# A four-layer image network on one core: layer 3's last sum one pair later, search's sum over its own row of norms, and the freed room as load buffers

## The chip, the cores and the metric

The kernel runs on one core of one Trainium2 chip. The metric is device time in microseconds (us), from the first to the last instruction with what lies around them; less is better. The core has five engines with an instruction stream each, executed in order: TensorE (PE, matmul; PEld is its weight load), VectorE (DVE), ScalarE (ACT), GpSimd (POOL) and SyncE (SP, which here only issues transfers). They meet through semaphores. Matmuls write to PSUM, a small memory of eight banks of 512 float32 per partition; everything else lives in SBUF, and large arrays in HBM.

## What is computed

Sixteen images of 64 x 64 tokens with 256 channels, in float32, go through four layers. Each normalises its input over 32 groups of channels (`_gn`), computes something and adds it to the input.

```python
# layer 0: nearest of 1024 codes
dis = sum(xf*xf) + sum(e*e) - 2*xf@e;  x = x + e.T[argmin(dis)]
# layer 1: attention within each row of 64 tokens, sigmoid instead of softmax
attn = sigmoid(einsum('bhik,bhjk->bhij', x@Wf+bf, x@Wg+bg));  x = x + attn @ (x@Wh+bh)
# layer 2: a gate per token from a softmax over 4096 tokens of a rank-one product
sim = x0[:, :, None]*x1[:, None, :];  feats = einsum('bn,bnm->bm', x2, softmax(sim, axis=1))
x = x + sigmoid(feats) * x
# layer 3: linear attention with 4 heads of 32, a projection, a layer norm over channels
q = softmax(q over d)*32**-0.5;  k = softmax(k over n)
out = (context(k, v) applied to q) @ w_out + b_out
x = x + layernorm(out)*gamma + beta
```

## The kernel before

Every image passes through stages, written as Python generators that yield after a piece of work: `stats0` (group statistics of the input), `stage1` (the search of layer 0), `layer1`, `rows2` and `stage2` (layer 2: its three rows, then the exponentials), `gate2` (the gate) and `stage3` (layer 3). A list of tasks with start times and lengths merges the generators of several images, so that the search of one image, layer 1 of another, the exponentials of a third, and gate and layer 3 of older ones run beside each other. That merged order only sets priorities: a tile library then schedules the instructions engine by engine by its own estimate of when each is ready, hands out the buffers of its pools, and puts in all semaphores. So the number of buffers under a tag sets not only what may be in flight but also the final order on each engine. Between stages the activations go through HBM, in chunks of 512 tokens (512 KB each; eight chunks per image).

What the change touches, with the line numbers of the profile:

- **The shared load buffers `xb`** (L57), three of them. Four stages load chunks into them on SP's queue: the statistics (xs, L293), the rows of layer 2 (xr, L562), the keys and values of layer 3 (xk, L732) and its output pass (xo, L846). `rows2` takes eight chunks in two halves of four; each chunk is read by two matmuls (L565); after a half, ACT copies the rows (L569), TensorE transposes them (L574) and DVE stores the two columns (L575) that `stage2` needs to begin.
- **The tag `t4`** in the pool `s1p`, five buffers of 4 KB per partition: the negated norms nn (L372), the sums nd (L384), the squares sq of the search's normalisation (L325), the projections fg of layer 1 (L464), the rows of layer 2 (L569), and a constant at the start.
- **The search** per token tile of 128: ACT forms nn = minus the norms (L372); TensorE makes the products with the 1024 codes in a two-bank PSUM tile pd (L377, four matmuls); DVE adds both into nd and takes the maximum (L384), then finds its place (L389, FIND_INDEX8); POOL gathers the code and adds it to the tokens (L390).
- **The gate** (`gate2`), per chunk: SP loads the chunk xg (L665) and a row gb of gates, the same for all partitions (L667, one buffer); ACT makes the factors u (L674), DVE multiplies (L675); SP stores (L681). The gates reach HBM by a transfer on ACT's queue (L641).
- **Layer 3's output pass**, per chunk of four tiles, two pairs each. `form` loads the queries qo (L824, tag `qo`, two buffers) and makes a product (L826, L828); `variance` reduces it to the layer norm's scale (L834, L836, L837). For each pair TensorE makes po (L854); ACT scales it into y (L857); TensorE transposes the input into the PSUM bank px and adds a row (L859, L863); DVE adds px and y (L865). When a chunk's second pair is done, the first pair of the next chunk stores it (L867; the last chunk at L872). The y tiles have two buffers.
- **PSUM**: the pool `ps_m` has four banks, taken in turn by nearly all small products of all stages (po, px, pz, pvr, pr, pt, pk, pqv, pfg, psc and more); `ps_w` has two double banks for pd, ph and po of layer 1.

Of the kernel before, what the change touches and what calls it, by code (L numbers as in the profile page):

```python
# [9 lines left out]
F32 = mybir.dt.float32  # L10
# [3 lines left out]
ALU = mybir.AluOpType  # L14
AX = mybir.AxisListType

P = 128
C = 256
NK = C // P
# [4 lines left out]
CW = CH * P  # L24
# [3 lines left out]
CODES = 1024  # L28
CK = 32
# [12 lines left out]
def kernel(  # L42
# [7 lines left out]
    nc = tc.nc  # L50
# [3 lines left out]
    const = ctx.enter_context(tc.tile_pool(name="const", bufs=1))  # L54
    xa = ctx.enter_context(tc.tile_pool(name="xa", bufs=3))
    xm = ctx.enter_context(tc.tile_pool(name="xm", bufs=3))
    xb = ctx.enter_context(tc.tile_pool(name="xb", bufs=3))  # L57
    xg = ctx.enter_context(tc.tile_pool(name="xg", bufs=2))
    s1p = ctx.enter_context(tc.tile_pool(name="s1p", bufs=2))
    s2p = ctx.enter_context(tc.tile_pool(name="s2p", bufs=1))  # L60
    s3p = ctx.enter_context(tc.tile_pool(name="s3p", bufs=2))
# [33 lines left out]
    dmat = const.tile([P, P], F32, name="dmat")  # L95
    nc.vector.tensor_tensor(dmat, ident, gmat, ALU.subtract)
    hmask = blocks("hmask", DH, 1.0)
    neg_mat = s1p.tile([P, P], F32, tag="t4", name="neg_mat", bufs=5)
    nc.vector.memset(neg_mat, -1.0)
    neg32 = const.tile([P, 32], F32, name="neg32")  # L100
    nc.vector.memset(neg32, -1.0)
# [201 lines left out]
    def stage1(b):  # L303
        tag = f"s1_{b}"
        scale, _, nbias = norm0.pop(b)
        src = xT[b].rearrange("(k p) n -> p k n", p=P)
        tok = x[b].rearrange("(t p) c -> p t c", p=P)
        xt, xc, xn, nx2, pxt = {}, {}, {}, {}, {}

        def load(ch):  # L310
            xt[ch] = xa.tile([P, NK, CW], F32, tag="xa", name=f"xt_{tag}_{ch}")
            nc.sync.dma_start(out=xt[ch], in_=src[:, :, ch * CW : (ch + 1) * CW])

        def tokens(ch):
            xc[ch] = s1p.tile([P, CH, C], F32, tag="xc", name=f"xc_{tag}_{ch}")
            nc.sync.dma_start(out=xc[ch], in_=tok[:, ch * CH : (ch + 1) * CH, :])

        def norm(ch):
            xn[ch] = s1p.tile([P, NK, CW], F32, tag="xn", name=f"xn_{tag}_{ch}")
            sq = s1p.tile([P, NK, CW], F32, tag="t4", name=f"sq_{tag}_{ch}", bufs=5)  # L320
            for k in range(NK):
                nc.scalar.activation(
                    xn[ch][:, k, :], xt[ch][:, k, :], AF.Identity, bias=nbias[:, k : k + 1], scale=scale[:, k : k + 1]
                )
                nc.scalar.activation(  # L325
                    sq[:, k, :], xt[ch][:, k, :], AF.Square, bias=nbias[:, k : k + 1], scale=scale[:, k : k + 1]
                )
            px = bank(f"px_{tag}_{ch}")
            for t in range(CH):
                for k in range(NK):  # L330
                    nc.tensor.matmul(
                        px[32 * t : 32 * t + 32, :P], lhsT=neg32, rhs=sq[:, k, t * P : (t + 1) * P],
                        start=(k == 0), stop=(k == NK - 1),
                    )
            xrow = small.tile([P, P], F32, tag="xrow", name=f"xrow_{tag}_{ch}", bufs=1)
            nc.scalar.copy(xrow, px[:, :P])
            pxt[ch] = bank(f"pxt_{tag}_{ch}")
            nc.tensor.transpose(pxt[ch][:, :P], xrow, ident)

        def norm_rows(ch):  # L340
            px = pxt.pop(ch)
            nx2[ch] = small.tile([P, CH], F32, tag="x2", name=f"nx2_{tag}_{ch}")
            nc.vector.tensor_copy(nx2[ch], px[:, :P].rearrange("p (t n) -> p t n", n=32)[:, :, 0])  # L343

        st1 = stats_tile(1, f"st1_{tag}")
        x1_d[b] = []

        def back(ch):
            for k in range(NK):
                pt = bank(f"pt_{tag}_{ch}_{k}")  # L350
                for t in range(CH):
                    nc.tensor.transpose(
                        pt[:, t * P : (t + 1) * P], xc[ch][:, t, k * P : (k + 1) * P], ident
                    )
                nc.scalar.copy(xt[ch][:, k, :], pt)
            chunk_stats(st1, xt[ch], ch)
            d = dram.tile([P, NK, CW], F32, tag=f"x1_{ch}", name=f"x1_{tag}_{ch}")
            nc.scalar.dma_start(out=d, in_=xt.pop(ch))
            x1_d[b].append(d)

        load(0)
        load(1)
        norm(0)
        norm_rows(0)
        tokens(0)
        yield 4
        for ch in range(NCHUNK):
            for t in range(CH):
                T = ch * CH + t

                nn = s1p.tile([P, CODES], F32, tag="t4", name=f"nn_{tag}_{T}", bufs=5)
                nc.scalar.activation(nn, ne2, AF.Identity, bias=nx2[ch][:, t : t + 1])  # L372
                pd = wide(f"pd_{tag}_{T}")
                for hf in range(2):
                    cols = slice(hf * 512, (hf + 1) * 512)
                    for k in range(NK):
                        nc.tensor.matmul(  # L377
                            pd[:, cols], lhsT=xn[ch][:, k, t * P : (t + 1) * P], rhs=e2[:, k, cols],
                            start=(k == 0), stop=(k == NK - 1),
                        )  # L380

                nd = s1p.tile([P, CODES], F32, tag="t4", name=f"nd_{tag}_{T}", bufs=5)
                m8 = m8s[T % 4]
                nc.vector.tensor_tensor_reduce(  # L384
                    out=nd, in0=pd, in1=nn, scale=1.0, scalar=-3.0e38, op0=ALU.add, op1=ALU.max,
                    accum_out=m8[:, 0:1],
                )
                i8 = small.tile([P, 8], U32, tag="i8", name=f"i8_{tag}_{T}", bufs=4)
                nc.vector.max_index(i8, m8, nd)  # L389
                nc.gpsimd.indirect_dma_start(  # L390
                    out=xc[ch][:, t, :], out_offset=None,
                    in_=emb_rows, in_offset=bass.IndirectOffsetOnAxis(ap=i8[:, 0:1], axis=0),
                    compute_op=ALU.add,
                )
# [21 lines left out]
    def layer1(b):  # L416
        tag = f"l1_{b}"
        scale, nmean, _ = norm1.pop(b)
# [32 lines left out]
        def attend(ch):  # L451
            X = xt[ch]
            pfg = bank(f"pfg_{tag}_{ch}")
            HW = CW // 2
            for k in range(NK):
                for n in range(4):
# [1 line left out]
                        pfg[n * CK : (n + 1) * CK, :HW], lhsT=wfg_n[:, k, (n // 2) * CK : (n // 2 + 1) * CK],  # L458
                        rhs=X[:, k, (n % 2) * HW : (n % 2 + 1) * HW], start=(k == 0), stop=(k == NK - 1),
                    )  # L460
            fg = s1p.tile([2 * CK, 2, HW], F32, tag="t4", name=f"fg_{tag}_{ch}", bufs=5)
            for n in range(2):
                part = slice(2 * n * CK, 2 * (n + 1) * CK)
                nc.scalar.activation(fg[:, n, :], pfg[part, :HW], AF.Identity, bias=bfg_n[part, :])  # L464
# [75 lines left out]
    def rows2(b):  # L540
        tag = f"r2_{b}"
        scale, nmean, _ = norm2[b]
# [15 lines left out]
        for h in range(2):  # L558
            pr = bank(f"pr_{tag}_{h}")
            for j in range(4):  # L560
# [3 lines left out]
                for k in range(NK):  # L564
                    nc.tensor.matmul(  # L565
                        pr[part, :], lhsT=wrow_n[:, k, part], rhs=xt[:, k, :], start=(k == 0), stop=(k == NK - 1)
                    )
            rows = s1p.tile([P, CW], F32, tag="t4", name=f"rows_{tag}_{h}", bufs=5)
            nc.scalar.activation(rows, pr, AF.Identity, bias=brow_n)  # L569
            for n in range(3):  # L570
                nc.scalar.dma_start(out=rd[n, h], in_=rows[n : n + 97 : 32, :])
# [81 lines left out]
    def gate2(b):  # L653
        tag = f"g2_{b}"
        scale, nmean, _ = norm2.pop(b)
# [7 lines left out]
        for ch in range(NCHUNK):  # L663
            xt = xg.tile([P, NK, CW], F32, tag="xg", name=f"xg_{tag}_{ch}")
            nc.sync.dma_start(out=xt, in_=x2[ch])  # L665
            gb = s3p.tile([P, CW], F32, tag="gb", name=f"gb_{tag}_{ch}", bufs=1)
            nc.sync.dma_start(  # L667
                out=gb,
                in_=gd[ch * CH : (ch + 1) * CH, :].rearrange("t p -> (t p)").rearrange("(o n) -> o n", o=1)
# [19 lines left out]
    def stage3(b):  # L689
# [130 lines left out]
        qs, prods, rss = {}, {}, {}  # L820

        def form(ch):
            qs[ch] = s3p.tile([P, CW], F32, tag="qo", name=f"qo_{tag}_{ch}")
            nc.sync.dma_start(out=qs[ch], in_=qTs[ch])  # L824
            pz = bank(f"pz_{tag}_{ch}")
            nc.tensor.matmul(pz, lhsT=gram, rhs=qs[ch], start=True, stop=True)  # L826
            prods[ch] = s3p.tile([P, CW], F32, tag="v2", name=f"qz_{tag}_{ch}", bufs=4)
            nc.vector.tensor_tensor(prods[ch], pz, qs[ch], ALU.mult)  # L828
# [11 lines left out]
        yield 3  # L840
        variance(0)
        yield 3
        before = None
        for ch in range(NCHUNK):
            xt = xb.tile([P, NK, CW], F32, tag="xb", name=f"xo_{tag}_{ch}")
            nc.sync.dma_start(out=xt, in_=x3[ch])  # L846
# [2 lines left out]
            for pr in range(2):  # L849
# [11 lines left out]
                            is_transpose=True, start=(j == 0 and k == 0), stop=False, skip_group_check=True,  # L861
                        )
                nc.tensor.matmul(px, lhsT=ones3, rhs=twice(x_row), start=False, stop=True, skip_group_check=True)  # L863
                two = y[:, 2 * pr : 2 * pr + 2, :]
                nc.vector.tensor_tensor(two, px, two, ALU.add)  # L865
                if pr == 0 and before is not None:
                    nc.sync.dma_start(out=dst[:, (ch - 1) * CH : ch * CH, :], in_=before)  # L867
                if ch + 1 < NCHUNK:
                    (form, variance)[pr](ch + 1)
                yield 3  # L870
            before = y
        nc.sync.dma_start(out=dst[:, TOK // P - CH :, :], in_=before)  # L872


# [70 lines left out]
```

## Time and profile before

| | us |
|---|---|
| median of three runs | 5931.24 (5928.14 to 5945.72) |
| the profiled execution, in all | 5928.44 |
| its span, first to last instruction | 5926.7 |
| ACT ex_s (L617), 1024 times | 2137.8, mean 2088 ns |
| DVE ex_s (L620), 1024 times | 2350.7, mean 2302 ns |
| PE pd_s (L377), 4096 times | 2022.2, mean 623 ns |
| DVE sum of the search (L384), 512 times | 622.2, mean 1215 ns |
| DVE FIND_INDEX8 (L389), 512 times | 624.1, mean 1219 ns |
| ACT nn_s (L372), 512 times | 583.2, mean 1141 ns |
| DVE sum of layer 3 (L865), 256 times | 175.2, mean 686 ns |
| POOL gather (L390), 512 times | 1058.1, mean 2067 ns |

The profile is one execution on the chip. Its page gives the busy time of each engine, the span in 40 slices (a digit is the busy share in tenths; PEclk is the clock granted to TensorE, in tenths of full speed), the transfer queues, the chain of work that ended last, and groups of instructions: line, engine, operation, tile written <- tiles read, count, busy time, mean ns of one, and the idle time of the engine ahead of them with what ended it. A wait is written as the waiting engine, tile and line, then `<-` and what released it. SPq is SP's queue of transfers. Matmuls are pipelined, so a busy TensorE is not one at its peak. TensorE's 4096 pd_s here are float32 matmuls that each stand as two instructions.

The first 500 us fill the pipeline of stages, the last 600 empty it; between, the picture repeats every 351 us.

### The profile page before, as it was taken

Reading aid. Unit: us, or ns where it says so; the run is one execution under the profiler, and the core shown is the slowest. Engines: PE = TensorE matmul, PEld = TensorE weight load, DVE = VectorE, ACT = ScalarE, POOL = GpSimd, SP = SyncE. Lnnn points to the kernel's source line nnn. Section 1 sums busy time; section 2 is a strip of 40 time slices with the busy share of each in tenths; the row PEclk is TensorE's granted clock in tenths of the full one; section 3 lists DMA queues with packets and bytes.
Section 4 is the critical chain, followed back from the end, with each engine's and each line's share of the span. In section 5 each row is a group of like instructions: output and inputs, shape, how many; then the busy total and the mean of one; then the engine's idle time right before and its main releaser. Section 6 shows DMA issues by size and latency. Waiting matters only on the chain.

```text
span 5926.7 us, 79561 instructions
## 1 busy us (share of the span) xinstructions
PE 5337.4 (90%) x28239; PEld 3211.1 (54%) x28239; DVE 5121.1 (86%) x7282; ACT 4570.8 (77%) x6754; POOL 1939.4 (33%) x1314
## 2 busy tenths in 40 slices
PE   8968899889999999998989999898999989997777
PEld 3524465545656565564656556565555646564555
DVE  6499798989989898898989889898998989888882
ACT  4377687878778787887879788797878878787873
POOL 3122233224233332433334233342424333231331
PEclk9989999989999898999999899999999999998899
DMA  6544745555656656565665656656565664644543
GB/s 186 162 124 124 225 137 177 184 184 162 207 168 192 197 151 202 184 207 181 184 205 167 194 183 188 206 174 204 164 210 164 202 204 147 209 158 173 184 158 116
DMA packets 521380, 1059.47 MB, mean 179 GB/s; under 512 B 52504, under 2 KB 266392, under 8 KB 512792
## 3 DMA queue, kind: packets, MB, share of 16 engines
q1 hardware_dynamic: 406288, 885.11, 44.7%
q0 software_dynamic: 73728, 67.14, 7.9%
q10 hardware_dynamic: 40968, 102.13, 4.5%
q8 instruction: 224, 3.67, 0.3%
q14 instruction: 172, 1.41, 0.1%
HBM read 751.18 MB, written 303.04 MB: 178 GB/s over the span
## 4 chain that ended last, share of the span: by engine, by line
PE 48%; DVE 16%; ACT 12%; DMA 7%; issue 6%; POOL 4%; ACTq 0%; SPq 0%; POOLq 0%; DVEq 0%
PE pd_s L377 15%; DVE ex_s L620 6%; ACT ex_s L617 5%; PE ph_l L468 5%; PE pqv_s L759 3%; PE po_s L854 3%; PE pk_s L737 3%; PE po_l L506 2%; PE pr_r L565 2%; DMA xr_r<-x_l 2%; DVE i_s L389 2%; POOL qv_s L779 2%; PE pvr_s L834 1%; PE pz_s L826 1%; DMA qo_s<-qd_s 1%
## 5 line engine op out<-in xcount | busy, mean ns | idle before, releaser
L620 DVE CUSTOM_DVE_ANT_0 ex_s<-ex_s,x2b 128x2048 f32<-128x2048 f32 x1024 | 2350.7, 2302 | 46.2 <-ACT ex_s L617 44.9
L617 ACT ACTIVATE ex_s<-x0b,nmax_s,x_r 128x2048 f32<-128x2048 f32 x1024 | 2137.8, 2088 | 66.4 <-DVE num_s L620 60.3
L377 PE MATMUL pd_s<-e,xn_s 128*128 128x512 f32 x4096 | 2022.2, 623 | 43.5 <-DVE m L384 40.8
L390 POOL DMA_INDIRECT xc_s<-in_emb_rows,i_s x512 | 1058.1, 2067 | 2063.9 <-DVE i_s L389 1466.8
L377 PEld LDWEIGHTS pd_s<-e,xn_s 128*128 128x128 f32 x4096 | 754.4, 197 | 764.9 <-issue 669.1
L384 DVE CUSTOM_DVE_ANT_0 nd_s<-pd_s,nn_s 128x1024 f32<-128x1024 f32 x512 | 622.2, 1215 | 174.4 <-ACT nn_s L372 82.1
L389 DVE FIND_INDEX8 i_s<-m,nd_s 128x8 uint32<-128x1024 f32 x512 | 624.1, 1219 | 0.0
L372 ACT ACTIVATE nn_s<-ne,nx_s 128x1024 f32<-128x1024 f32 x512 | 583.2, 1141 | 21.5 <-DVE nx_s L343 15.7
L468 PE MATMUL ph_l<-wh_l,xt_l 128*128 128x256 f32 x2048 | 525.5, 393 | 28.3 <-DVE m L384 16.5
L759 PE MATMUL pqv_s<-wqv_s,xk_s 128*128 128x256 f32 x2048 | 494.6, 382 | 0.0
L759 PEld LDWEIGHTS pqv_s<-wqv_s,xk_s 128*128 128x128 f32 x2048 | 390.9, 192 | 127.5 <-issue 65.5
L468 PEld LDWEIGHTS ph_l<-wh_l,xt_l 128*128 128x128 f32 x2048 | 380.9, 193 | 143.8 <-issue 57.5
L837 POOL TENSOR_TENSOR lrs_s<-lrs_s,mhalf 128x4 f32<-128x4 f32 x128 | 183.0, 1429 | 749.3 <-ACT lrs_s L836 710.5
L857 ACT ACTIVATE y_s<-po_s,lrs_s 128x256 f32<-128x256 f32 x512 | 237.1, 469 | 214.8 <-PE po_s L854 166.2
L854 PE MATMUL po_s<-wctx_s,qo_s 128*128 128x256 f32 x1024 | 336.0, 415 | 32.3 <-ACT y_s L857 31.1
L506 PE MATMUL po_l<-at_l,h_l 64*128 64x64 f32 x4096 | 318.5, 297 | 46.2 <-DVE xt_l L511 42.7
L506 PEld LDWEIGHTS po_l<-at_l,h_l 64*128 64x128 f32 x4096 | 286.5, 206 | 108.5 <-DVE xt_l L511 48.9
L779 POOL TENSOR_TENSOR qv_s<-qv_s,qm_s 128x512 f32<-128x512 f32 x128 | 232.7, 1818 | 312.3 <-DVE qm_s L778 181.7
L728 POOL TENSOR_TENSOR qv_s<-qv_s,qd_s 128x512 f32<-128x512 f32 x128 | 199.8, 1561 | 304.6 <-DVE qd_s L727 252.9
L865 DVE TENSOR_TENSOR y_s<-pxo_s,y_s 128x512 f32<-128x512 f32 x256 | 175.2, 686 | 125.0 <-ACT y_s L857 123.2
L854 PEld LDWEIGHTS po_s<-wctx_s,qo_s 128*128 128x128 f32 x1024 | 178.2, 198 | 172.5 <-ACT y_s L857 84.7
L737 PE MATMUL pk_s<-xk_s,wk_s 128*128 128x512 f32 x512 | 269.6, 650 | 0.0
(195 smaller groups left out, 7519.8 us busy)
## 6 DMA issues: line engine op xcount, KB each, us to landing
xs_s<-in_xT SPq DMA_DIRECT2D x128, 512.0 KB
xt_s<-in_xT SPq DMA_DIRECT2D x128, 512.0 KB
xc_s<-in_x SPq DMA_DIRECT2D x128, 512.0 KB
x_s<-xt_s ACTq DMA_DIRECT2D x128, 512.0 KB
xt_l<-x_s SPq DMA_DIRECT2D x128, 512.0 KB
x_l<-xt_l SPq DMA_DIRECT2D x128, 512.0 KB
xr_r<-x_l SPq DMA_DIRECT2D x128, 512.0 KB
xg_g<-x_l SPq DMA_DIRECT2D x128, 512.0 KB
```

Of the source, the lines that this page charges most:

```text
L372: nc.scalar.activation(nn, ne2, AF.Identity, bias=nx2[ch][:, t : t + 1])
L377: nc.tensor.matmul(pd[:, cols], lhsT=xn[ch][:, k, t * P : (t + 1) * P], rhs=e2[:, k, cols], start=(k == 0), stop=(k == NK - 1),)
L384: nc.vector.tensor_tensor_reduce(out=nd, in0=pd, in1=nn, scale=1.0, scalar=-3.0e38, op0=ALU.add, op1=ALU.max, accum_out=m8[:, 0:1],)
L389: nc.vector.max_index(i8, m8, nd)
L390: nc.gpsimd.indirect_dma_start(out=xc[ch][:, t, :], out_offset=None, in_=emb_rows, in_offset=bass.IndirectOffsetOnAxis(ap=i8[:, 0:1], axis=0),
L468: nc.tensor.matmul(ph[:, t, :], lhsT=X[:, k, t * P : (t + 1) * P], rhs=wh_n[:, k, :], start=(t % 2 == 0 and k == 0), stop=False, skip_grou ...
L506: nc.tensor.matmul(po[:, r, k * CH + t, :], lhsT=h[rows, t, k * P : (k + 1) * P], rhs=at[rows, t, :], start=True, stop=True,)
L617: nc.scalar.activation(ex, x0b, AF.Exp, bias=nmax[:, T : T + 1], scale=x01[:, T, 1:2], accum_out=den[:, h, T : T + 1])
L620: nc.vector.tensor_tensor_reduce(out=ex, in0=ex, in1=x2b, scale=1.0, scalar=0.0, op0=ALU.mult, op1=ALU.add, accum_out=num[:, h, T : T + 1],)
L737: nc.tensor.matmul(pk, lhsT=wk_n[:, k, :], rhs=xt[:, k, :], start=(k == 0), stop=(k == NK - 1))
L759: nc.tensor.matmul(pqv[:, j, :], lhsT=xt[:, k, t * P : (t + 1) * P], rhs=wqv_n[:, k, :], start=(j == 0 and k == 0), stop=False, skip_group ...
L854: nc.tensor.matmul(po[:, j, :], lhsT=qT[:, t * P : (t + 1) * P], rhs=wctx[:, 1, :], start=True, stop=True)
```

## The change

Five edits, all in one function:

1. `xb` gets a fourth buffer.
2. The search's sum is written over nn, so that nd goes; the tag `t4` goes from five buffers to three. FIND_INDEX8 reads nn.
3. The gate row gb gets a second buffer.
4. The query tile qo gets a third buffer.
5. In layer 3's output pass the sum of px and y of a pair is issued after the matmuls of the next pair (`late`); the store of the previous chunk moves from the first pair to the second; the very last sum stands after the loop.

In SBUF, per partition: `t4` gives back 8 KB; xb takes 4, gb and qo 2 each.

```diff
-    xb = ctx.enter_context(tc.tile_pool(name="xb", bufs=3))
+    xb = ctx.enter_context(tc.tile_pool(name="xb", bufs=4))
...
-            sq = s1p.tile([P, NK, CW], F32, tag="t4", name=f"sq_{tag}_{ch}", bufs=5)
+            sq = s1p.tile([P, NK, CW], F32, tag="t4", name=f"sq_{tag}_{ch}", bufs=3)
...
-                nn = s1p.tile([P, CODES], F32, tag="t4", name=f"nn_{tag}_{T}", bufs=5)
+                nn = s1p.tile([P, CODES], F32, tag="t4", name=f"nn_{tag}_{T}", bufs=3)
...
-                nd = s1p.tile([P, CODES], F32, tag="t4", name=f"nd_{tag}_{T}", bufs=5)
                 m8 = m8s[T % 4]
                 nc.vector.tensor_tensor_reduce(
-                    out=nd, in0=pd, in1=nn, scale=1.0, scalar=-3.0e38, op0=ALU.add, op1=ALU.max,
+                    out=nn, in0=pd, in1=nn, scale=1.0, scalar=-3.0e38, op0=ALU.add, op1=ALU.max,
                     accum_out=m8[:, 0:1],
                 )
...
-                nc.vector.max_index(i8, m8, nd)
+                nc.vector.max_index(i8, m8, nn)
...
-            gb = s3p.tile([P, CW], F32, tag="gb", name=f"gb_{tag}_{ch}", bufs=1)
+            gb = s3p.tile([P, CW], F32, tag="gb", name=f"gb_{tag}_{ch}", bufs=2)
...
-            qs[ch] = s3p.tile([P, CW], F32, tag="qo", name=f"qo_{tag}_{ch}")
+            qs[ch] = s3p.tile([P, CW], F32, tag="qo", name=f"qo_{tag}_{ch}", bufs=3)
...
-        before = None
+        before = late = None
         for ch in range(NCHUNK):
...
                 nc.tensor.matmul(px, lhsT=ones3, rhs=twice(x_row), start=False, stop=True, skip_group_check=True)
-                two = y[:, 2 * pr : 2 * pr + 2, :]
-                nc.vector.tensor_tensor(two, px, two, ALU.add)
-                if pr == 0 and before is not None:
+                if late is not None:
+                    nc.vector.tensor_tensor(late[1], late[0], late[1], ALU.add)
+                late = px, y[:, 2 * pr : 2 * pr + 2, :]
+                if pr == 1 and before is not None:
                     nc.sync.dma_start(out=dst[:, (ch - 1) * CH : ch * CH, :], in_=before)
                 if ch + 1 < NCHUNK:
                     (form, variance)[pr](ch + 1)
                 yield 3
             before = y
+        nc.vector.tensor_tensor(late[1], late[0], late[1], ALU.add)
         nc.sync.dma_start(out=dst[:, TOK // P - CH :, :], in_=before)
```

The buffer count of `t4` changes from 5 to 3 in the same way at the constant, at fg and at the rows.

More of the change, by code (lines that the diff above doesn't have):

```diff
@@ L97 @@
     hmask = blocks("hmask", DH, 1.0)
-    neg_mat = s1p.tile([P, P], F32, tag="t4", name="neg_mat", bufs=5)
+    neg_mat = s1p.tile([P, P], F32, tag="t4", name="neg_mat", bufs=3)
     nc.vector.memset(neg_mat, -1.0)
@@ L460, in attend @@
                     )
-            fg = s1p.tile([2 * CK, 2, HW], F32, tag="t4", name=f"fg_{tag}_{ch}", bufs=5)
+            fg = s1p.tile([2 * CK, 2, HW], F32, tag="t4", name=f"fg_{tag}_{ch}", bufs=3)
             for n in range(2):
@@ L567, in rows2 @@
                     )
-            rows = s1p.tile([P, CW], F32, tag="t4", name=f"rows_{tag}_{h}", bufs=5)
+            rows = s1p.tile([P, CW], F32, tag="t4", name=f"rows_{tag}_{h}", bufs=3)
             nc.scalar.activation(rows, pr, AF.Identity, bias=brow_n)
```

## The prediction

> **What bounds the kernel now.** I read the page first, then the span cut into stretches, then the waits of TensorE in the steady part, then the waits of SP's own queue, then the chain of waits around one change of image and at the end. Parts 1 and 2 of the page:
>
> ```profile
> PE 5337.4 (90%) x28239; PEld 3211.1 (54%) x28239; DVE 5121.1 (86%) x7282; ACT 4570.8 (77%) x6754; POOL 1939.4 (33%) x1314
> PE   8968899889999999998989999898999989997777
> ...
> PEclk9989999989999898999999899999999999998899
> ```
>
> No engine is idle for long. The steady part repeats every 351 us (one image leaves, one enters). Two of its stretches, with a column each for PE, PEld, DVE, ACT and POOL busy, the granted clock, the DMA share and GB/s:
>
> ```profile
> 2400.00:2750.00 350.00, 325.32 (x1781) 197.76 (x1780) 320.96 (x458) 288.88 (x426) 125.15 (x81) 0.98 0.61 190
> 3450.00:3800.00 350.00, 327.57 (x1756) 199.02 (x1756) 316.11 (x447) 283.62 (x419) 122.54 (x80) 0.96 0.60 186
> ```
>
> TensorE is busy 93% of it and leaves some 23 us per image. Finer stretches show that these lie around the change of image:
>
> ```profile
> 3740.00:3760.00 20.00, 18.26 (x64) 8.62 (x67) 20.00 (x26) 14.75 (x26) 8.80 (x7) 0.78 0.36 111
> 3760.00:3780.00 20.00, 16.48 (x59) 5.62 (x54) 16.04 (x24) 13.39 (x16) 3.19 (x3) 0.91 0.61 181
> 3780.00:3800.00 20.00, 16.92 (x71) 8.49 (x70) 15.48 (x25) 14.15 (x22) 6.07 (x4) 1.00 0.93 335
> ```
>
> There all three engines are short of work at once, and the clock is granted at 0.78. What TensorE waits for from 2400 to 4850 us, seven images (us in total, times, longest):
>
> ```profile
> PE pr_r L565 <- DMA xr_r<-x_l: 31.7, 14, 3.9
> PE po_l L506 <- DVE xt_l L511: 27.0, 7, 3.9
> PE px_s L331 <- ACT sq_s L325: 25.4, 27, 2.8
> PE pz_s L826 <- DMA qo_s<-qd_s: 13.5, 6, 3.6
> ```
>
> The first and fourth are loads that come late; the second and third the change does not touch. Why the loads are late stands in SP's queue, over the whole run:
>
> ```profile
> SPq L667 <- ACT u_g L674: 433.3, 86, 14.1
> ...
> SPq L732 <- PE pqv_s L763: 310.0, 62, 16.2
> ...
> SPq L562 <- PE pr_r L565: 262.7, 56, 16.3
> ```
>
> Each is a load at the head of an in-order queue that waits until the last reader of a buffer is done: L667 the single gate row, L732 and L562 the three shared load buffers. Whatever stands behind it waits too. The chain of waits at one change of image, and in the last 60 us:
>
> ```profile
> 3761.57 3.48 DMA xr_r<-x_l
> ...
> 3778.78 6.54 DMA xr_r<-x_l
> ```
>
> ```profile
> 5876.02 4.83 DMA qo_s<-qd_s
> ...
> 5897.58 3.78 DMA qo_s<-qd_s
> ...
> 5904.31 3.71 DMA qo_s<-qd_s
> ```
>
> Summed over its whole length, the chain spends 132.5 us in loads xr (L562), 83.8 in qo (L824), 43.3 in xs (L293) and 30.6 in gb (L667): 290 us, the ceiling for the three added buffers.
>
> **What the Trainium skill says.** "DMA: Bandwidth & Descriptors", section "Anatomy of one DMA": a semaphore wait happens on the issuing sequencer before dispatch, so a load for which no buffer is free holds its queue. The trace agrees, with the 433.3 us above. "TensorE: Matmul & The Clock Gate", section "What's actually happening": an idle TensorE falls to half clock and needs sustained work to rise again. It agrees here: at 3755.32 us six pd_s matmuls took 4.38 us on the chain (730 ns each), where eight took 3.43 (429 ns) in the calm part. "Perfetto Trace Analysis", section "Optimization Strategy": the same gap repeating on the engine that should be full can mean too few buffers. The 23 us per image are such a gap.
>
> **The change part by part.** Each engine executes the same instructions as before (none added, none removed); what changes is buffers, and the order. I read the order in the changed program as it was built.
>
> *Fourth buffer xb.* Before, image 9's rows loads stand in SP's queue as xr 0, store, token load, xr 1, xr 2, four other transfers and more, xr 3: the fourth waits for the first's two matmuls. Changed, the four of the first half stand within six places and the four of the second half one behind the other. TensorE's waits for xr are 54.6 us in the whole run. Gain between 0 (bandwidth: the core moved 335 GB/s from 3780 to 3800, so more loads at once may only share it) and 54.6; I take two thirds, 36, because the second half's loads must still follow the first half's matmuls. The xs loads (layer norm statistics of the next image) are 43.3 us of chain, but TensorE never waits for them and DVE only 13.3 us: I take 5, between 0 and 13.
>
> *Third query tile.* The loads qo stand one chunk earlier. In the last 60 us nothing else is left to run, so the 4.83, 3.78 and 3.71 us of the chain should go: 12. Elsewhere TensorE waits 21.7 - 4.9 (its part after 5400 us) = 16.8 us; I take two thirds, 11. Together 23, between 0 and 29. The first query load of an image waits for the write of the same data by ACT's queue, which the tile does not help.
>
> *Second gate row.* Of the 30.6 us of gb on the chain, those behind a gd store (L641) stay; 4.66, 6.03 and 6.40 us at 582, 606 and 5525 us could go. In the steady part ACT never waits for gb, so SP's freed 433 us only let other loads go sooner. I take 10, between 0 and 17.
>
> *Late sum.* 256 instructions L865 (686 ns) move behind the next pair's matmuls. DVE's wait for ACT's y, 123.2 us (81 times), should nearly vanish, since y(n) is by then long done. But DVE is not the bound: in the steady part it is 38.6 us over seven images beside a busy TensorE. 56.6 us of it fall into the last 527 us, where DVE is as busy as PE or more up to 5700. The chain has 45.5 us of ACT y. I take 15, between 0 and 45. Behind the moved sum on DVE stand ex, nd and the statistics; they start sooner. The store L867 moves one pair later on SP; the y buffer it frees is next written 8 us or more after the store in the images I followed, and a pair in the tightest place takes 2.9 us, so I price it at nothing; were that cover gone, each of 128 chunks could lose up to those 2.9 us. What it does add: the PSUM bank of px stays taken for one pair more, in a pool of four banks that po, pz, the variance and all other stages share. No row shows this. From below nothing; from above one sum for each pair, 256 x 0.686 = 176 us, if TensorE waits each time. I take a tenth, 18, since the scheduler hands out banks knowing of the longer hold, and TensorE can run pd_s, which has other banks (wide pool).
>
> *Search's sum in place, t4 from five buffers to three.* Two of five tiles per token tile become one of three, held until FIND_INDEX8 ends: from the times of nn (L372) and of that instruction, the median hold grows from 5.0 to 7.4 us. Placing every nn, sq and fg tile of the trace into three buffers, only 12 of some 770 would have found none free, for 12.4 us in all on ACT; an nn never starts before the index search three tiles back has ended (closest 1.5 us). ACT is 77% busy and mostly ahead, so I take 4, between 0 and 12. DVE's time should not change: ex (L620) already works in place at 1.12 ns per element (2302 ns / 2048), the search's sum at 1.19 (1215 / 1024) from PSUM.
>
> *Clock.* Each removed stall also saves slow matmuls behind it: at 3755 six cost 6 x 0.30 = 1.8 us too much, at 3765 four pr matmuls took 3.06 us where four took 1.92 at 3785. That is 3 us per image at most, 48 over sixteen; since only some stalls go, 15, between 0 and 48.
>
> Sum: 36 + 5 + 23 + 10 + 15 + 15 = 104 gained, 18 + 4 = 22 lost, net 82. The profiled execution's span of 5926.7 becomes 5844.7; with the 1.7 us around it (5928.4 in all) 5846.4. The median of the runs is 2.8 above that execution, so 5849.
>
> **The rivals.** *Hidden anyway* (0.18): the loads come sooner, but TensorE at 93% then waits for po_l, px and pt instead, whose waits are as long; only the tail's 12 of qo and some 10 more remain: about 5909. For it: the waits 27.0 and 25.4 above sit in the same stretches. Against it: the xr stalls also hold ACT (rows_r, 113.0 us) and DVE (x_r, 110.8 us). *All of it* (0.20): the loads vanish, 200 of the ceiling of 290 is realised as the boundary closes, 48 of clock comes with it partly: net about 185, 5746. For it: all engines dip together there. Against it: DVE is 90% and PE 93% busy. *PSUM runs short* (0.17, slower): px's bank, held over the next pair, leaves po, px and pz of the next pair and one more; every other stage's small matmuls queue behind a DVE sum. If TensorE waits one sum for each pair, 176 + 12 for t4 against 104 gained: +84, 6015. It decides from 104 / 256 = 0.4 us a pair. For it: TensorE already waits 31.1 us for ACT's y at po (L854). Against it: only some 110 us of each 351 contain these pairs. *It does not do what it says*: the built order shows the loads ahead, so only their landing can fail; that is the first rival.
>
> **How the numbers follow.** Forecast 0.45, 5849; its own range is 5800 to 5900. Hidden 0.18, all 0.20, short 0.17. Anything within 0.3% (18 us) I call no change, about what a measurement of this kernel can tell. Faster: 0.45 + 0.20 + about half of hidden and a little of short, 0.75; the same 0.09; slower 0.16. The range 5745 to 5930 takes in most of all but the last.
>
> **What would show it.** TensorE's wait for xr under 25 us and for qo under 10; SP's wait at the gate row for ACT u far below 433; DVE's wait for y under 30; the 20 us stretches at the change of image above 18 us of PE busy and their clock above 0.9; FIND_INDEX8 still 1219 ns. I am wrong if po, pxo or pt_s begin to wait for DVE's y sum, if ACT's nn waits for the index search, or if the xr loads only take longer each.

## The result, and the profile after

| | before | changed |
|---|---|---|
| median, four runs each | 5929.69 us (5914.35 to 5945.72) | 5832.52 us (5826.67 to 5844.59) |
| ratio, 95% interval | | 0.9838 (0.9807 to 0.987) |
| profiled execution, in all | 5928.44 | 5844.59 |
| its span | 5926.7 | 5842.9 |

The change takes off 97 us, where 82 were forecast. (The profiled execution of the changed kernel is the slowest of its four.) The first part of the page of the changed kernel, and its rows of TensorE's and the clock's tenths:

```profile
PE 5282.9 (90%) x28239; PEld 3202.0 (55%) x28239; DVE 5119.0 (88%) x7282; ACT 4570.5 (78%) x6754; POOL 1981.5 (34%) x1314
...
PE   8978899889999899999999999999998999997788
...
PEclk9988999989999999999999999999999999998889
```

The instruction counts are the same and DVE and ACT are as busy as before. TensorE is not: its busy time fell by 54.5 us (from 5337.4). Of the 83.8 us by which the two spans differ, then, 54.5 are *busy* time and only 29.3 idle time, although the change removes waits. Two groups of TensorE's instructions explain that. Columns: line, instruction, count, then busy us, mean ns, idle us before them and what ended it. Before:

```profile
L565 PE MATMUL pr_r<-xr_r,wrow_n 128*32 128x512 f32 x512 | 168.5, 659 | 55.0 <-DMA xr_r<-x_l 54.6 <-ACT brow_r L555 0.3
```

Changed (the line numbers are one less from here on, since the line of nd is gone):

```profile
L564 PE MATMUL pr_r<-xr_r,wrow_n 128*32 128x512 f32 x512 | 113.1, 642 | 4.5 <-DMA xr_r<-x_l 4.1 <-ACT brow_r L554 0.4
```

The wait for the loads xr is gone, as forecast: 54.6 to 4.1 us. But the same 512 matmuls, of nearly the same mean length (659 and 642 ns), also fill 55.4 us less. They must lie beside each other. The timeline shows it; columns are start, length, engine, line, instruction, count, and in brackets the idle time before. One change of image before:

```profile
3759.63 1.93 PE L565 MATMUL pr_r<-xr_r,wrow_n 128*32 128x512 f32 x12
3765.08 3.06 PE L565 MATMUL pr_r<-xr_r,wrow_n 128*32 128x512 f32 x4 [3.52 <-DMA xr_r<-x_l]
...
3785.36 1.90 PE L565 MATMUL pr_r<-xr_r,wrow_n 128*32 128x512 f32 x4 [0.39 <-DMA xr_r<-x_l]
...
3787.31 0.69 ACT L569 ACTIVATE rows_r<-pr_r,brow_r 128x512 f32<-128x512 f32 x1 [4.69 <-PE pr_r L565]
```

and changed:

```profile
3702.60 1.93 PE L564 MATMUL pr_r<-xr_r,wrow_n 128*32 128x512 f32 x12
...
3712.25 1.94 PE L564 MATMUL pr_r<-xr_r,wrow_n 128*32 128x512 f32 x16
...
3714.37 0.69 ACT L568 ACTIVATE rows_r<-pr_r,brow_r 128x512 f32<-128x512 f32 x1 [0.94 <-PE pr_r L564]
```

Sixteen of them take 1.94 us, and so do twelve; four alone take 1.90. The loop writes four strips of 32 partitions of one PSUM bank, one strip for each chunk (`128*32` in the rows is the shape of the weights), and by these records strips whose data are there run side by side. The Trainium skill states as much: "TensorEngine Tiling (Array Packing)", section "Tiling Modes", lists 128x32 as four tiles of the array, and says that different tiles can execute matmuls in parallel. The trace agrees, with 1.94 us for sixteen against 1.90 for four. A chunk that lands late therefore costs its wait *and* a full 1.9 us on its own. The ends of matmuls are modelled, but ACT's copy of the bank, which waits for the last of them, starts 2.12 us after the first of the sixteen, and 1.95 us after the first of the lone four.

With three buffers the four chunks of a half can never all be there, since the fourth load waits for the first chunk's matmuls. In the traces of all seven kernels here with three load buffers, no stretch of pr_r holds more than twelve of them; in all seven with four buffers, stretches of sixteen occur. Before, the 512 matmuls stand in 83 stretches; changed, in 58, with 17 of the 32 halves whole. All 32 whole would be 62 us busy (32 x 1.94, an estimate), so 113.1 is not the end of it.

The idle time has moved more than it shrank. Among TensorE's longest waits before, with total us, times and longest:

```profile
PE px_s L331 <- ACT sq_s L325: 63.7, 54, 5.5
PE pt_s L352 <- DMA xc_s<-in_emb_rows,i_s: 57.1, 21, 8.3
PE pr_r L565 <- DMA xr_r<-x_l: 54.6, 25, 4.7
PE pg_n L259 <- DVE mv_n L256: 42.9, 19, 11.5
PE po_l L506 <- DVE xt_l L511: 42.7, 11, 4.6
PE pd_s L377 <- DVE m L384: 40.8, 28, 6.0
```

and changed:

```profile
PE pt_s L352 <- DMA xc_s<-in_emb_rows,i_s: 77.3, 28, 5.9
PE pg_n L259 <- DVE mv_n L256: 67.4, 19, 8.9
PE pd_s L377 <- DVE m L383: 54.8, 37, 6.7
PE pxt_s L338 <- ACT xrow_s L336: 37.0, 39, 5.5
...
PE px_s L331 <- ACT sq_s L325: 22.4, 27, 1.9
```

Three loads or stalls go almost wholly (xr 50.5 us less, po_l for DVE's xt_l 41.0, qo 21.7), px_s loses 41.3, and pt_s (now the longest: it waits for POOL's gathered codes), pg_n, pd_s, pxt_s and others take back most of it: all waits of TensorE together go from 578 to 550 us. SP's own queue, changed:

```profile
...
SPq L731 <- PE pqv_s L762: 353.2, 56, 19.9
...
SPq L666 <- ACT u_g L673: 238.0, 65, 17.4
...
SPq L867 <- DVE y_s L864: 222.3, 76, 6.2
...
SPq L561 <- PE pr_r L564: 163.6, 27, 11.4
```

The wait for the gate row falls from 433.3 to 238.0, that for xr from 262.7 to 163.6, and the store of the output, a pair later, waits longer (114.6 before). The change of image, in 20 us stretches, changed:

```profile
3680.00:3700.00 20.00, 17.92 (x44) 8.57 (x45) 18.06 (x24) 11.55 (x21) 6.83 (x7) 0.71 0.44 137
3700.00:3720.00 20.00, 19.07 (x78) 7.68 (x77) 19.18 (x25) 15.53 (x20) 5.33 (x3) 1.00 0.81 284
3720.00:3740.00 20.00, 19.37 (x81) 10.10 (x81) 17.11 (x34) 17.08 (x24) 4.08 (x4) 1.00 0.78 270
```

TensorE is busy above 19 us in the stretch that holds most of the pr_r matmuls and in the next (16.5 and 16.9 before), but the clock still falls to 0.71 in the one where they begin; the mean clock of the profiled execution is 0.941 before and 0.943 now (0.943 to 0.947 over the four timings). From the first image's first ex_s (on ACT) to the last image's, 15 steps, the time falls from 5175.7 to 5092.1 us, 5.6 for each image; the tail after it falls from 451.0 to 442.9, and the stretch ahead of it grows from 300.0 to 307.9.

### The profile page after: what moved, and what is told of

Read it like the earlier page. It is cut to its first block, busy times and chain, and to the rows that moved or that the text cites. A ratio compares the mean times of both kernels' runs of the same rounds, so it can differ in the third digit from the quotient of the medians.

```text
span 5842.9 us, 79478 instructions
## 1 busy us (share of the span) xinstructions
PE 5282.9 (90%) x28239; PEld 3202.0 (55%) x28239; DVE 5119.0 (88%) x7282; ACT 4570.5 (78%) x6754; POOL 1981.5 (34%) x1314
## 4 chain that ended last, share of the span: by engine, by line
PE 38%; DVE 18%; ACT 10%; issue 6%; DMA 4%; POOL 3%; ACTq 0%; POOLq 0%; SPq 0%; DVEq 0%
PE pd_s L377 12%; DVE ex_s L619 7%; ACT ex_s L616 5%; PE po_s L853 3%; PE ph_l L467 3%; PE po_l L505 2%; DVE i_s L388 2%; PE pqv_s L758 2%; PE pk_s L736 2%; POOL qv_s L778 2%; PE pz_s L825 1%; PE pvr_s L833 1%; PE pxo_s L858 1%; DMA x0b<-rows_r 1%; DVE st_s L249 1%
## 5 line engine op out<-in xcount | busy, mean ns | idle before, releaser
L619 DVE CUSTOM_DVE_ANT_0 ex_s<-ex_s,x2b 128x2048 f32<-128x2048 f32 x1024 | 2368.4, 2319 | 84.7 <-ACT ex_s L616 83.6
L389 POOL DMA_INDIRECT xc_s<-in_emb_rows,i_s x512 | 1158.7, 2263 | 1743.7 <-DVE i_s L388 1143.2
L377 PEld LDWEIGHTS pd_s<-e,xn_s 128*128 128x128 f32 x4096 | 766.9, 200 | 841.0 <-issue 696.6
L383 DVE CUSTOM_DVE_ANT_0 nn_s<-pd_s,nn_s 128x1024 f32<-128x1024 f32 x512 | 621.7, 1216 | 188.0 <-PE pd_s L377 88.9
L388 DVE FIND_INDEX8 i_s<-m,nn_s 128x8 uint32<-128x1024 f32 x512 | 624.8, 1221 | 0.0
L836 POOL TENSOR_TENSOR lrs_s<-lrs_s,mhalf 128x4 f32<-128x4 f32 x128 | 165.5, 1293 | 745.7 <-ACT lrs_s L835 723.4
L778 POOL TENSOR_TENSOR qv_s<-qv_s,qm_s 128x512 f32<-128x512 f32 x128 | 203.1, 1587 | 348.1 <-DVE qm_s L777 149.4
L505 PEld LDWEIGHTS po_l<-at_l,h_l 64*128 64x128 f32 x4096 | 274.5, 195 | 74.9 <-issue 37.2
L352 PE MATMUL pt_s<-ident,xc_s 128*128 128x128 f32 x1024 | 161.9, 287 | 107.1 <-DMA xc_s<-in_emb_rows,i_s 77.3
L736 PE MATMUL pk_s<-xk_s,wk_s 128*128 128x512 f32 x512 | 256.2, 624 | 0.0
```

The costliest lines, as they stand in the source:

```text
L377: nc.tensor.matmul(pd[:, cols], lhsT=xn[ch][:, k, t * P : (t + 1) * P], rhs=e2[:, k, cols], start=(k == 0), stop=(k == NK - 1),)
L383: nc.vector.tensor_tensor_reduce(out=nn, in0=pd, in1=nn, scale=1.0, scalar=-3.0e38, op0=ALU.add, op1=ALU.max, accum_out=m8[:, 0:1],)
L388: nc.vector.max_index(i8, m8, nn)
L389: nc.gpsimd.indirect_dma_start(out=xc[ch][:, t, :], out_offset=None, in_=emb_rows, in_offset=bass.IndirectOffsetOnAxis(ap=i8[:, 0:1], axis=0),
L505: nc.tensor.matmul(po[:, r, k * CH + t, :], lhsT=h[rows, t, k * P : (k + 1) * P], rhs=at[rows, t, :], start=True, stop=True,)
L619: nc.vector.tensor_tensor_reduce(out=ex, in0=ex, in1=x2b, scale=1.0, scalar=0.0, op0=ALU.mult, op1=ALU.add, accum_out=num[:, h, T : T + 1],)
```

## The experiments

Twelve kernels, each timed against the kernel before on the same chip, in five rounds. The theories that the expectations name: LOADS, the prediction's own, that the late loads (xr first) carry the gain at the prices given; SUM, that the late sum of layer 3 carries it; REORDER, that any of the edits changes the scheduler's order on all engines, and that this alone is worth tens of us of either sign; PLACE, that the search's sum over nn has a large price of its own.

| | kernel | median us | ratio to before, 95% |
|---|---|---|---|
| 1 | sum in place alone, `t4` 3 | 6086.21 | 1.0275 (1.0249 to 1.0301) |
| 2 | late sum alone | 5951.88 | 1.0028 (1.0016 to 1.0041) |
| 3 | changed, without the late sum | 5881.84 | 0.992 (0.9899 to 0.994) |
| 4 | 1 with a fourth load buffer | 5912.08 | 0.9973 (0.9961 to 0.9985) |
| 5 | sum in place alone, `t4` 5 | 6088.54 | 1.0267 (1.0243 to 1.029) |
| 6 | changed, two query tiles | 5855.31 | 0.9874 (0.9852 to 0.9895) |
| 7 | changed, one gate row | 5839.55 | 0.985 (0.9827 to 0.9873) |
| 8 | before, another lag | 5995.81 | 1.0109 (1.0087 to 1.0132) |
| 9 | changed, three load buffers | 5957.61 | 1.005 (1.0033 to 1.0068) |
| 10 | changed, another lag | 5823.09 | 0.9823 (0.98 to 0.9846) |
| 11 | sum apart, `t4` 4, fourth load buffer, late sum | 5965.68 | 1.0081 (1.0057 to 1.0104) |
| 12 | 1 with another lag | 6047.54 | 1.021 (1.0187 to 1.0232) |

**The edits one on top of the other.** 1 is the sum in place and `t4` at three; 4 adds the load buffer; 3 adds the gate row and the query tile; the changed kernel adds the late sum. 2 is the late sum without the rest.

```diff
1 (in part):
-                nn = s1p.tile([P, CODES], F32, tag="t4", name=f"nn_{tag}_{T}", bufs=5)
+                nn = s1p.tile([P, CODES], F32, tag="t4", name=f"nn_{tag}_{T}", bufs=3)
...
-                nd = s1p.tile([P, CODES], F32, tag="t4", name=f"nd_{tag}_{T}", bufs=5)
...
-                    out=nd, in0=pd, in1=nn, scale=1.0, scalar=-3.0e38, op0=ALU.add, op1=ALU.max,
+                    out=nn, in0=pd, in1=nn, scale=1.0, scalar=-3.0e38, op0=ALU.add, op1=ALU.max,
4: 1 and
-    xb = ctx.enter_context(tc.tile_pool(name="xb", bufs=3))
+    xb = ctx.enter_context(tc.tile_pool(name="xb", bufs=4))
```

> Kernel of before with edit 2 alone: search's sum over nn, t4 with three buffers, the freed 8 KB left empty. Theory LOADS (the gain of 97 us comes from the added load buffers; sharing t4 costs little): between -5 and +12 us against before, ACT's nn waits for the index search (L388) up to 12 us in all, FIND_INDEX8 stays at 1219 ns. Theory SUM (the gain comes from the late sum): the same here. Theory REORDER (most of the gain is that the scheduler happened upon a better order, and any change of buffers shifts the time by some tens of us): this kernel moves by over 20 us although it gets no buffer and no shorter instruction.

> Kernel of before with edits 2 and 1: in-place sum, three t4, and the fourth xb; gb one, qo two, sum not late. LOADS as in the prediction (xr 36, xs 5, part of the clock 10, t4 -4): about -45 us against before; TensorE's wait for xr under 15 us, that for qo still about 20. SUM: within 15 us of before.

> The changed kernel without edit 5 (in-place sum, three t4, four xb, two gb, three qo; layer 3's sum where it was). LOADS: 5835 to 5860, that is 70 to 95 us below before; DVE's wait for y stays near 120 us; TensorE's waits for xr and qo gone as in the changed kernel. SUM: 5900 or more.

> Kernel of before with edit 5 alone: layer 3's sum one pair later, all buffers as before. LOADS: -15 to +5 us (the saved waits of DVE for y, 123 us, lie beside a busy TensorE, and the PSUM bank held longer takes some back); TensorE's waits for xr and qo stay near 55 and 22 us. SUM: -60 to -97 us. In both, DVE's wait for ACT's y falls from 123 to about 30 us.

| step | forecast | measured |
|---|---|---|
| sum in place, `t4` 5 to 3 | +4 | +154 |
| fourth load buffer, on top | -41, and some clock | -174 |
| gate row and query tile, on top | -33 | -30 |
| late sum, on top | +3 (18 - 15) | -49 |
| late sum alone, on the kernel before | +3 | +20 |

Of the theories only REORDER left room for the first row (over 20 us), and the second is four times LOADS' price. Against before, LOADS had some -45 us for 4 and SUM within 15; it is -20. For 3, LOADS had 5835 to 5860 and SUM 5900 or more; it is 5881.84. So neither holds as it stands. The granted clock goes with the times: as a mean over each kernel's runs it is 0.940 before, 0.930 in 1, 0.939 in 4 and in 3, 0.945 in the changed kernel. So part of the first, the second and the fourth step may be clock; whether as a cause or as a consequence of fewer stalls, these runs do not tell.

What TensorE does with pr_r in 1 and in 4:

```profile
L564 PE MATMUL pr_r<-xr_r,wrow_n 128*32 128x512 f32 x512 | 162.3, 666 | 62.6 <-DMA xr_r<-x_l 62.0 <-ACT brow_r L554 0.3
```

```profile
L564 PE MATMUL pr_r<-xr_r,wrow_n 128*32 128x512 f32 x512 | 101.3, 633 | 1.7 <-DMA xr_r<-x_l 0.7 <-ACT y_s L856 0.6 <-ACT brow_r L554 0.3
```

The buffer removes 61.3 us of wait and 61.0 us of lost overlap, 122 of the 165.3 us by which the two profiled spans differ.

In 2 the stall of po_l behind xt_l falls from 42.7 to 1.3 us, in 3 it is 41.5 and in the changed kernel 1.7: under this lag it comes and goes with the late sum, with or without the buffers. DVE's wait for ACT's y falls too (123.2 us before, 53.8 in 2, 30.1 changed), but it is not the cause of the stall: in the trace of before, none of it lies beside one of the eleven waits of po_l. DVE is at work in all of them. The one at 3732 us:

```profile
3730.81 2.28 DVE L620 CUSTOM_DVE_ANT_0 ex_s<-ex_s,x2b 128x2048 f32<-128x2048 f32 x1
...
3733.02 0.68 DVE L865 TENSOR_TENSOR y_s<-pxo_s,y_s 128x512 f32<-128x512 f32 x1
...
3734.82 1.20 DVE L511 TENSOR_TENSOR xt_l<-po_l,xt_l 128x1024 f32<-128x1024 f32 x1
...
3736.08 2.18 PE L506 MATMUL po_l<-at_l,h_l 64*128 64x64 f32 x18 [3.85 <-DVE xt_l L511]
```

and the same place in the changed kernel:

```profile
3670.34 0.69 DVE L864 TENSOR_TENSOR y_s<-pxo_s,y_s 128x512 f32<-128x512 f32 x1
...
3671.61 0.38 PE L858 MATMUL pxo_s<-ident,xo_s 128*128 128x128 f32 x2
...
3672.13 1.22 DVE L510 TENSOR_TENSOR xt_l<-po_l,xt_l 128x1024 f32<-128x1024 f32 x1
...
3674.47 0.39 PE L265 MATMUL pv_n<-d_n,gmat 128*128 128x2 f32 x2 [1.30 <-ACT nm_n L269]
3674.79 1.54 PE L505 MATMUL po_l<-at_l,h_l 64*128 64x64 f32 x12
```

DVE goes through the same work ahead of xt_l, the sum of y included. What differs is TensorE's order: other matmuls now stand ahead of po_l, and one of them, pv_n, waits in its turn (for ACT's nm_n 0.3 us over the run before, 20.2 changed). So at this place the late sum works through the order, not through DVE's wait for y. In 8 below, another order alone brings the stall to 10.1 us, with the sum issued at once, and that kernel is slower.

Alone the late sum loses 20 us, where LOADS had -15 to +5 and SUM -60 to -97. The loads come sooner in 2 (TensorE's wait for xr 23.5 us, for qo 7.7, where near 55 and 22 were expected), but TensorE's idle time is as before (584 us of the span; 589 before), its busy time 34 us longer, 12 of that in pr_r, which stands in 99 stretches now. Why the same edit gains 49 us on top of the buffers is open; in the profiles of 3 and of the changed kernel the spans differ by 32.7 us, 24.9 of it idle time.

**Is it the three buffers?** 5 keeps the sum in place and gives `t4` its five buffers back (against 1; the other tiles of `t4` in the same way).

```diff
-                nn = s1p.tile([P, CODES], F32, tag="t4", name=f"nn_{tag}_{T}", bufs=3)
+                nn = s1p.tile([P, CODES], F32, tag="t4", name=f"nn_{tag}_{T}", bufs=5)
```

> Kernel of before with search's sum over nn, but t4 left at five buffers; nothing else. e1 (the same with three) was 154 us slower than before without one wait of nn for the index search. Theory THREE (three shared buffers make the scheduler put nn, sq, fg and rows later in ACT's order): within 20 us of before, about 5930. Theory PLACE (the in-place sum itself, whatever the room): near e1, 6050 to 6090. Theory REORDER (the order is a matter of luck): anything between, or outside.

5 is as slow as 1: THREE falls, and PLACE's number is met. The missing buffers do cause waits: ACT's waits in the changed kernel include

```profile
ACT nn_s L372 <- DVE i_s L388: 20.9, 20, 4.1
...
ACT sq_s L325 <- DVE i_s L388: 12.4, 9, 2.4
```

and in 5 both are gone. Since 1 (15.8 and 11.5 us of them) and 5 (none) take the same time, these waits cost nothing that shows. By the tiles that they write and read, the traces of 1 and 5 have 98% of ACT's and 99% of DVE's instructions in the same order; before and 1 have 84 and 88%. So the sum in place brings another order with it, and PLACE and REORDER are not told apart yet.

**How much is order worth?** 8, 10 and 12 change one number that only shifts where layer 3's task begins in the merged list: in the kernel before, in the changed one, and in 1.

```diff
-LAG4 = 0.04
+LAG4 = 0.045
```

> A measure of the order alone: the kernel of before with LAG4 0.045 for 0.04, which lets layer 3 of every image begin about 2 us later in the merged list of priorities; no buffer, instruction or wait is added. If the order is robust, within 10 us of before (5920 to 5942). REORDER: 20 us or more away, and then differences of this size between any two kernels here can't be put down to one buffer without a wait that shows it.

> The changed kernel with the lag of layer 3's task list at 0.045 instead of 0.04, which changes only the order in which work is merged. LOADS: with the loads no longer late the kernel has slack against its order, under +20 us, 5833 to 5853. REORDER: the order is worth tens of us here as well, as it was +63 us for the kernel before: +40 us or more, 5873 to 5930.

> The sum in place alone, three buffers of 4 KB, with the lag at 0.045 instead of 0.04: the same data dependences as the sum in place alone, in another order. PLACE (the dependence itself costs some 155 us): 6080 or more, and 80 above the kernel before with the same lag (5996). REORDER (the cost came with one order): under 6050, within 50 us of the kernel before with the same lag.

Without any edit of buffers or work, the kernel before loses 63 us to another order, and the sum in place gains 39. So the sum in place costs +154 us under one lag and +52 (6047.54 - 5995.81; by the ratios to before, as the two ran on different chips, some 60) under the other. A cost of the instruction or of its dependence would be there under both; some two thirds of the 154 belong to the order that came with it. PLACE's 6080 is missed; of REORDER's two numbers the first held (under 6050), the second just failed (within 50 us of 8). Whether the 52 to 60 are order too is open. The changed kernel takes no harm from the new lag (-9 us, intervals overlapping): REORDER's +40 was wrong for it, and LOADS' 5833 to 5853 a little high. That fits loads that have slack, though one other order is a small sample.

**The terms taken out one at a time.** 6, 7 and 9 undo one buffer each in the changed kernel.

```diff
6:
-            qs[ch] = s3p.tile([P, CW], F32, tag="qo", name=f"qo_{tag}_{ch}", bufs=3)
+            qs[ch] = s3p.tile([P, CW], F32, tag="qo", name=f"qo_{tag}_{ch}", bufs=2)
7:
-            gb = s3p.tile([P, CW], F32, tag="gb", name=f"gb_{tag}_{ch}", bufs=2)
+            gb = s3p.tile([P, CW], F32, tag="gb", name=f"gb_{tag}_{ch}", bufs=1)
9:
-    xb = ctx.enter_context(tc.tile_pool(name="xb", bufs=4))
+    xb = ctx.enter_context(tc.tile_pool(name="xb", bufs=3))
```

> The changed kernel with the query tile back at two buffers (the room left empty). By the prediction's 23 us for the third tile: 5850 to 5860, with TensorE's wait for qo back near 20 us, and the loads qo back in the last 60 us of the chain. If REORDER rules, a difference of either sign that doesn't go with the wait for qo.

> The changed kernel with one gate row. By the prediction's 10 us: 5838 to 5848; SP's wait at the gate row for ACT's u back from 238 towards 430 us; in the steady part no difference. REORDER: a difference of over 20 us of either sign.

> The changed kernel with three shared load buffers instead of four; all other edits stay. LOADS (the prediction's own price, 36 + 5 us): 5874, TensorE's wait for the xr loads back at some 4 us per image. PLACE (the sum in place costs some 155 us and the fourth load buffer is what pays for it, as it took 174 us off the sum in place): 5990 or more. REORDER (the gain is of the order alone, no price of its own): anything from 5850 to 6000, with the xr wait back but not equal to the difference.

6: 23 us, the forecast's very number, though the two intervals overlap a little. In its profile the tail after the last image's first ex_s is 454.0 us against 442.9, 11 of the 12 forecast for the last images' query loads; TensorE's wait for qo is 4.7 us in place of none, where some 20 were expected. The other half can't be pointed to, as the two profiled spans differ by 10.5 us in all. 7: 7 us, with intervals that overlap: 10 were forecast, nothing is excluded between none and that. SP's wait at the gate row, expected back near 430, is 248.3 us with the one row, so its fall from 433.3 to 238.0 is not the second row's doing.

9: without the fourth load buffer the changed kernel is slower than the kernel before. The buffer is worth 125 us here (5957.61 - 5832.52), three times its price. LOADS' 5874 and PLACE's 5990 are both missed; the result lies in REORDER's wide range. Its profile:

```profile
L564 PE MATMUL pr_r<-xr_r,wrow_n 128*32 128x512 f32 x512 | 160.0, 667 | 48.1 <-DMA xr_r<-x_l 48.1
```

Against the changed kernel that is 44.0 us more wait and 46.9 us more busy time in one group, 91 of the 117.6 us by which the profiled spans differ. The wait alone gives 44, the pair 91; the rest was not located, and an order that changes with the buffer can have a part in all of it, as in every step here.

**A version that keeps the sum apart.** If the sum in place really cost 154 us, dropping it should win. 11 fits the room: `t4` at four with nd, four load buffers, the late sum, gate row and query tile as before.

```diff
-    xb = ctx.enter_context(tc.tile_pool(name="xb", bufs=3))
+    xb = ctx.enter_context(tc.tile_pool(name="xb", bufs=4))
...
-                nd = s1p.tile([P, CODES], F32, tag="t4", name=f"nd_{tag}_{T}", bufs=5)
+                nd = s1p.tile([P, CODES], F32, tag="t4", name=f"nd_{tag}_{T}", bufs=4)
...
-                if pr == 0 and before is not None:
+                if late is not None:
+                    nc.vector.tensor_tensor(late[1], late[0], late[1], ALU.add)
+                late = px, y[:, 2 * pr : 2 * pr + 2, :]
+                if pr == 1 and before is not None:
```

> The search's sum in a buffer of its own as before, with four buffers of 4 KB instead of five; four shared load buffers; the late sum; one gate row and two query tiles, as before. It fills the same room as the kernel before. LOADS (prediction's terms: the load buffer 41, the late sum 15 - 18, clock some 10): about 5885. PLACE (the sum in place is itself worth -155 us that the changed kernel still pays): well under the changed kernel, 5700 to 5790. REORDER: 5800 to 5900, with neither sign certain.

It is slower than the kernel before, and 133 us slower than the changed one, of which the query tile and the gate row, by 6 and 7, account for some 30. None of the three forecasts holds. PLACE's is the farthest off: beside a fourth load buffer no burden of the sum in place shows. TensorE's wait for xr is gone in 11 (1.6 us), yet pr_r is busy 136.5 us. It stands in 80 stretches, 40 of them of two matmuls, and only 4 halves are whole: other matmuls stand between the strips in TensorE's order, though the loads are in time. Whether the rest of the 103 us is the room (ACT's sq again keeps px_s waiting, 55.0 us over the run) or the order was not told apart. Of all kernels tried only 10 lies below the changed one, by less than the intervals tell apart.

## Why the prediction was right, and where not

The total, 5849 for 5832.5, and the sign are right; several terms of the sum are not. Two large errors cancel, the sum in place (154 us lost in 1, where 4 were reckoned) and the fourth buffer (174 gained on top of it, where 41 were). That they do so this nearly is luck: the prediction had no reason for it.

- **Fourth buffer xb, 36 and 5 us.** The mechanism is right: the wait fell by 50.5 of 54.6 us. The size is not: 125 us in the changed kernel (9). The term priced the wait and left out the lost overlap of the strips, 46.9 us in the same run, although the prediction itself says that "the fourth waits for the first's two matmuls": with three buffers that holds for every half.
- **Clock, 15.** The line is read rightly as far as it goes: "at 3765 four pr matmuls took 3.06 us where four took 1.92 at 3785", and the granted clock is 0.50 from 3765.8 to 3769 us, behind an idle time of 3.52 us. (At 3755, the prediction's other example, only 0.50 us of idle time stands ahead of the slow matmuls.) What was not seen beside it is that twelve take 1.93. Whether the clock gained is open. The stretch at the change of image still falls to 0.71 with TensorE busy 17.92 us, where above 0.9 and 18 were expected, and in the two profiles TensorE's work without pr_r is as long as before (5168.9 and 5169.8 us). But the profiled execution has the lowest clock of the changed kernel's four, which average 0.945, and the timings of the kernel before average 0.940 on the chips of the experiments. From these two, an estimate: 0.005 of 5832 us, 29 us if TensorE were busy all the time.
- **Third query tile, 23.** Measured 23 (6), with 11 of it located, in the tail.
- **Second gate row, 10.** Measured 7, not distinguishable from nothing (7).
- **Late sum, 15 gained, 18 lost.** DVE's wait for y fell to 30.1 us (28.2 at L864, 1.9 at the very last sum), about the 30 expected. But "the second and third the change does not touch" failed: po_l for DVE's xt_l falls by 41.0 us, px_s for ACT's sq by 41.3. Nor are "all three engines" short of work at 3740: the line shown there has DVE busy for all 20.00 us. On top of the buffers the edit is worth 49 us (3), alone it costs 20 (2); neither is the term's 15, and what it does to the order was not in the sum. The PSUM bank's 18 never showed: TensorE waits for DVE's y sum neither before nor in the changed kernel (2.0 us in 2), and the rival that made it dear is out.
- **Sum in place, 4.** DVE's instructions are as long as before (FIND_INDEX8 1221 ns), as said. ACT's nn does wait for the index search, 20.9 us, and sq 12.4, where 12.4 were reckoned for all; the first was named as a sign of being wrong, but 5 shows no cost of it. What costs 154 us alone, and 52 to 60 under another lag, is for the most part the order that came with the edit, a term that the sum didn't have.

*Hidden anyway* was half right: waits of TensorE did move elsewhere, all but 28 us. Two thirds of the gain between the profiles, 54.5 of 83.8 us, come from the busy time, which that rival didn't look at. *All of it* asked for 185 us and was too high.

## What to carry to other kernels

When matmuls into separate strips of one bank can run side by side, a late operand costs more than its wait: compare the busy time of the group with count times mean, and ask what it would be with everything there, and whether there are buffers enough for everything to be there at once. Where a scheduler orders the work, an edit of a buffer count also draws a new order, here worth up to 63 us with no edit of work or buffers at all; so a single edit's time is not its price until it has been measured on top of the others, or under a second order. Prices of such edits don't add: the late sum was +20 alone and -49 on top of the buffers. And a wait of one engine is not the cause of another's because both shrink together: look at what the engine named was doing at that time.

## What was not expected of the hardware

That the four strips of pr_r overlap almost wholly (1.94 us for sixteen, 1.90 for four) the prediction had not reckoned with. The edited DVE instructions ran as the profile of before said: the sum over its own input 1216 ns where the sum into another tile took 1215, and FIND_INDEX8 1221 against 1219. Others grew a little: DVE's ex_s from 2302 to 2319 ns, POOL's gather from 2067 to 2263 (spans on POOL are rough).
